# A cross-attention and gated feed-forward kernel: instruction order at the start, the queues of the attention results, and the form of the down projection

## The chip, the cores and the metric

The kernel runs on one core of a Trainium2 chip. A core has a matrix engine (TensorE, PE in the profile, with its weight loads as PEld), a vector engine (VectorE, DVE), an activation engine (ScalarE, ACT), a general engine (GpSimd, POOL) and a queue engine (SyncE, SP). Each runs its own instructions in order and waits for the others by semaphores. DMAs are issued from the instruction streams of SP, ACT or POOL: an instruction that waits there holds back everything behind it, DMAs among them. The metric is the device time of one execution, in microseconds (us).

## What is computed

Eight sequences of 128 tokens with 512 features, all float32: cross attention with 32 heads of 128, then a feed-forward block with 1376 inner features.

```
h   = rmsnorm(layernorm(x)) * ln_weight
q, k, v = h @ w_q.T, ctx @ w_k.T, ctx @ w_v.T          # 32 heads x 128 each
p   = softmax(q k^T + position_bias, masked)
x1  = x + layernorm(x) + (p v) @ w_out.T
y   = layernorm(x1)
g   = silu((y @ Wg.T) * ag) * ((y @ Wu.T) * au)         # 1024 x 1376
out = x1 + (g @ Wd.T) * ad                              # 1024 x 512
```

## The kernel before

**Products.** A float32 matrix product takes two passes through PE, so each matmul in the code stands as two instructions in the profile. Nearly all projections use a seven-product scheme: both operands are cut in 2 x 2 blocks, seven products of sums of blocks replace eight of blocks. The sums of the left operand are made by `sums_a` (L215, four operations: `s1`, `s2`, a difference written over `a21`, and `s4`), those of the right by `sums_b` (L223: `t1`, `t2`, a difference over `b12`, and `t4`). `combine_rows` (L231) makes the sums of a weight tile on GpSimd, `combine_tokens` (L239) those of the tokens on VectorE, with `b12` on GpSimd. `seven` (L248) yields once for each product and tile, in the order 2, 1, 6, 7, 4, 5, 3 with two tiles each, so 14 times; products 2, 6, 7 and 4 are copied out by ScalarE (L259, L269), 1, 5 and 3 added by VectorE (L264, L275). Product 6 needs `s2` and `t2`, product 7 the differences over `a21` and `b12`.

**Start.** The loads are issued by hand on SP and ACT (L131 to L147). `kv(0)` (L396) makes the keys and values of the first of eight groups of four heads, 28 yields; between them the loop at L417 runs `norm1` (L183) and `norm1_T` (L202) for each block of 128 tokens. `norm1` takes mean and variance, a reciprocal deviation, the normed row `y` on VectorE, its square sum on ScalarE, a second reciprocal deviation and the scaled row `hn`; `norm1_T` transposes it on PE into `hT`. The queries of all eight groups follow (L437) and are stored in DRAM.

**Attention.** For each group g and block b, `probabilities` (L316) adds bias and mask on GpSimd (L320), the scores on VectorE (L328), and does the softmax on DVE and ACT. `transpose_p` (L355) turns p by a 32 x 32 transpose on DVE (L358), one DMA to DRAM (`turned`, L360) and four back (`pT`, L365), all on SP. Three blocks later `attend` (L377) multiplies with the values, copies by ScalarE (L386) and writes `att` to DRAM by SP (L387). Meanwhile PE makes the next group's keys and values. In the last group PE does the output projection of the first pair of blocks instead: `out_products(0)` takes a step for each group, after `attended(g, 0)` (L478) has loaded `att` back into `a` (L480, SP) and made its sums on DVE; `load_wo` (L455) loads the output weights and makes their sums on GpSimd. The other three pairs follow (L640), their loads also by `attended`.

**Feed-forward.** Five slices of 256 inner features go through `seven` for gate and up (L724), with the weight sums on GpSimd and `gated` (L687) for the slice before; the last 96 features are done plainly in `last_slice`. Each 128 inner features have an `act` tile. The down projection (L762) is plain: for each block of tokens 11 matmuls of 512 columns, then two operations on VectorE (times `ad`, plus `x1`) and a write; the last block is done in two halves.

**Order.** The kernel's text gives priorities; the framework's scheduler orders each engine's and queue's instructions by its own estimate of when each is ready. `InOrder` (L37) pins an instruction behind all that are traced before it on its engine; before the change, it is used for PE in the last group (which is why those matmuls are all recorded at L45). Tiles of a pool with the same tag share its buffers: `acts` has 18, `work` has several tags with two to four.

Of the kernel before, what the change touches and what calls it, by code (L numbers as in the profile page):

```python
# [17 lines left out]
P = 128  # L18
# [31 lines left out]
def xattn_ffn_kernel(  # L50
# [97 lines left out]

    lnw_sb = const.tile([P, DC], F32, name="lnw_sb")
# [33 lines left out]
    def norm1(b):  # L183
        st = small.tile([P, nc.vector.BN_STATS_DIM], F32, tag="st", name=f"st_{b}")
        xb = x_in[b // 2][:, b % 2, :]
        moments(mv1, b, st, xb)
        rs = rs1[:, b : b + 1]
        rstd_of(rs, mv1[:, b, 1:2], 1.0)
        y = work.tile([P, D], F32, tag="s", name=f"y_{b}", bufs=3)
        nc.vector.tensor_scalar(  # L190
            y, xb, mv1[:, b, 0:1], rs, ALU.subtract, ALU.mult
        )
        sq = work.tile([P, D], F32, tag="aT", name=f"sq_{b}")
        ss = small.tile([P, 1], F32, tag="ss", name=f"ss_{b}")
        nc.scalar.activation(sq, y, AF.Square, accum_out=ss)
        rr = small.tile([P, 1], F32, tag="rr", name=f"rr_{b}")
        rstd_of(rr, ss, 1.0 / D)
        hn = work.tile([P, D], F32, tag="pT", name=f"hn_{b}", bufs=4)
        nc.scalar.activation(hn, y, AF.Copy, scale=rr)
        return b, hn  # L200

    def norm1_T(b, hn):  # L202
        tp = transposed(hn, ps_tp.tile([P, DC, P], F32, tag="pt", name="tp"))
        nc.vector.tensor_tensor(
# [26 lines left out]
    def combine_rows(name, w):  # L231
# [5 lines left out]
        return sums_a(nc.gpsimd, a11, a12, a21, a22, s1, s2, s4)  # L237

    def combine_tokens(src):  # L239
# [6 lines left out]
        return sums_b(nc.vector, b11, b12, b21, b22, t1, t2, t4, nc.gpsimd)  # L246

    def seven(name, tiles, product, part, pool, tag="mm"):  # L248
# [13 lines left out]
        for t in tiles:  # L262
            product(1, t, m[t], True)
            nc.vector.tensor_tensor(part(1, 1, t), part(1, 1, t), m[t], ADD)  # L264
            yield
# [6 lines left out]
        for i, r, c in ((5, 2, 2), (3, 1, 2)):  # L272
            for t in tiles:
                product(i, t, m[t], i == 5)
                nc.vector.tensor_tensor(part(r, c, t), part(r, c, t), m[t], ADD)  # L275
                yield
# [100 lines left out]
    def attend(g, b, pT, v):  # L377
# [9 lines left out]
        nc.sync.dma_start(att[g][b // 2][:, b % 2], aT)  # L387
# [8 lines left out]
    def kv(g, out):  # L396
# [3 lines left out]
        keys = project_T(f"k{g}", combine_rows(f"k{g}", wk), ctx_t, kT)  # L400
# [3 lines left out]
        else:  # L404

            yield from itertools.islice(keys, 4)
            values = project_V(f"v{g}", combine_rows(f"v{g}", wv), ctx_t, v, ps, "sc")
            yield from itertools.islice(values, 4)
            yield from keys
# [4 lines left out]
    ctx_t = combine_tokens(ctx_sb)  # L414
    kvs = {}
    normed = []
    for n, _ in enumerate(kv(0, kvs)):  # L417
        if n % 2 == 1 and 5 <= n < 5 + 2 * B:
            normed.append(norm1((n - 5) // 2))
        if n % 2 == 1 and 11 <= n < 11 + 2 * B:  # L420
            norm1_T(*normed.pop(0))
    for n in normed:
        norm1_T(*n)
    h_t = combine_tokens(hT)

    res_scale = const.tile([P, B], F32, name="res_scale")
    res_bias = const.tile([P, B], F32, name="res_bias")
    nc.vector.tensor_scalar_add(res_scale, rs1, 1.0)
# [391 lines left out]
```

## Time and profile before

| | us |
|---|---|
| median of three runs | 1146.57 (1145.29 to 1150.09) |
| the profiled execution | 1144.65 |
| its span in the profile | 1142.9 |

The profile shows one execution. Where its time goes, by stages of the span (busy us of each engine):

| stage | from, to | PE | DVE | ACT | POOL |
|---|---|---|---|---|---|
| first loads, first product | 0 to 10.91 | 5.7 | 0.7 | 1.0 | 2.5 |
| keys, values, first norm | 10.91 to 68.25 | 50.9 | 33.3 | 23.4 | 30.3 |
| queries | 68.25 to 260.5 | 192.3 | 36.9 | 38.8 | 43.0 |
| attention, groups 0 to 6 | 260.5 to 700 | 438.3 | 258.3 | 187.0 | 152.0 |
| last group, first output pair | 700 to 780 | 70.9 | 49.5 | 19.0 | 28.7 |
| other output pairs | 780 to 926.9 | 146.9 | 52.2 | 9.7 | 14.1 |
| gate and up | 926.9 to 1063.3 | 135.5 | 60.8 | 38.7 | 27.8 |
| down projection | 1063.3 to 1142.9 | 75.8 | 13.5 | 0.1 | 0.0 |

Matmuls are pipelined and their ends are modelled, so a busy PE is not always at its full rate: the time from one start to the next tells the rate. Waits are put down to what came last by semaphore. In groups of waits, the columns are the total, how often, and the longest; in a timeline, the start and the duration.

### The profile page before, as it was taken

How to read it: one execution, taken by the hardware profiler on the slowest of the kernel's cores; microseconds unless marked ns; L12 is line 12 of the kernel's file. 1: busy time of each engine (PE TensorE's matmuls, PEld its weight loads, DVE VectorE, ACT ScalarE, POOL GpSimd, SP SyncE). 2: the span in 40 equal slices, each digit the busy share in tenths (PEclk: the TensorE clock that was granted, in tenths of full speed). 3: DMA queues.
4: the chain of work that ended last, by engine and by line, in shares of the span. 5: the costliest groups of instructions: out<-in, count | busy, mean ns of one | idle time of the engine just before them, and what ended most of it. 6: DMA issues, size and time to landing. Idle time of an engine off the chain costs nothing.

```text
span 1142.9 us, 12312 instructions
## 1 busy us (share of the span) xinstructions
PE 1116.1 (98%) x4286; PEld 729.4 (64%) x4286; DVE 505.2 (44%) x957; ACT 317.5 (28%) x899; POOL 298.4 (26%) x255
## 2 busy tenths in 40 slices
PE   7899999999999999999999999889999999999998
PEld 3564444445867778685868679778888864444445
DVE  4541111116555565555555767653434342434311
ACT  2511112223343444443443443221000022233000
POOL 5531221116333333332311633510000314220000
PEclk9999999999999999999999999989999999999999
DMA  9114433257646555565555466765232602110000
GB/s 281 47 37 146 177 119 111 110 183 263 181 133 208 157 184 167 175 194 168 178 166 165 144 193 217 228 198 159 90 104 63 227 8 74 37 37 1 18 28 28
DMA packets 117533, 154.38 MB, mean 135 GB/s; under 512 B 12032, under 2 KB 71680, under 8 KB 117472
## 3 DMA queue, kind: packets, MB, share of 16 engines
q1 hardware_dynamic: 114784, 149.93, 41.0%
q10 hardware_dynamic: 2192, 2.10, 0.6%
q0 software_dynamic: 496, 1.58, 0.5%
q8 instruction: 34, 0.56, 0.2%
q14 instruction: 27, 0.22, 0.1%
HBM read 101.14 MB, written 52.43 MB: 134 GB/s over the span
## 4 chain that ended last, share of the span: by engine, by line
PE 90%; DVE 4%; DMA 3%; ACT 1%; issue 1%; POOL 0%; SPq 0%; ACTq 0%; DVEq 0%; POOLq 0%
PE mm_q L285 17%; PE mm_v L303 16%; PE mm_k L285 14%; PE m L500 13%; PE mm_f L739 9%; PE dn L770 7%; PE sc L325 4%; PE m L45 4%; PE av L381 4%; DMA a<-att 1%; DMA wv<-in_wvT_dram 1%; ACT s L335 1%; PE av L45 1%; PE tp L176 1%; PE gp L704 1%
## 5 line engine op out<-in xcount | busy, mean ns | idle before, releaser
L320 POOL TENSOR_TENSOR s<-pb,mneg 128x512 f32<-128x512 f32 x64 | 81.6, 1275 | 278.9 <-DVE tt L358 238.6
L285 PE MATMUL mm_k<-ctx_sb,wk 128*128 128x512 f32 x256 | 119.4, 610 | 8.8 <-DMA wk<-in_wkT_dram 4.7
L303 PE MATMUL mm_v<-wv,ctx_sb 128*128 128x256 f32 x512 | 115.9, 379 | 0.5 <-DMA wv<-in_wvT_dram 0.5
L285 PE MATMUL mm_q<-hT,wq 128*128 128x512 f32 x256 | 112.5, 592 | 0.0
L335 ACT ACTIVATE s<-s,nmx 128x128 f32<-128x128 f32 x256 | 99.5, 390 | 34.5 <-DVE nmx L332 34.5
L303 PEld LDWEIGHTS mm_v<-wv,ctx_sb 128*128 128x128 f32 x512 | 95.3, 190 | 14.5 <-DMA wv<-in_wvT_dram 1.3
L386 ACT COPY aT<-av 128x512 f32<-128x512 f32 x64 | 37.5, 585 | 210.9 <-issue 125.4
L285 PE MATMUL mm_k<-ctx_sb,S_k 128*128 128x512 f32 x192 | 87.2, 598 | 3.6 <-POOL S_k L218 2.6
L285 PEld LDWEIGHTS mm_q<-hT,wq 128*128 128x128 f32 x256 | 48.6, 190 | 60.8 <-issue 60.7
L285 PEld LDWEIGHTS mm_k<-ctx_sb,wk 128*128 128x128 f32 x256 | 47.6, 195 | 62.5 <-issue 42.1
L303 PE MATMUL mm_v<-S_v,ctx_sb 128*128 128x256 f32 x384 | 86.7, 381 | 0.0
L285 PE MATMUL mm_q<-hT,S_q 128*128 128x512 f32 x192 | 85.0, 592 | 0.0
L328 DVE TENSOR_TENSOR s<-sc,s 128x512 f32<-128x512 f32 x64 | 44.1, 689 | 85.6 <-PE sc L325 73.8
L303 PEld LDWEIGHTS mm_v<-S_v,ctx_sb 128*128 128x128 f32 x384 | 71.6, 190 | 10.5 <-DVE v L275 1.5
L770 PE MATMUL dn<-wd,act 128*128 128x512 f32 (+3 forms) x198 | 75.8, 545 | 0.0
L275 DVE TENSOR_TENSOR q<-q,mm_q 128x512 f32<-128x512 f32 x32 | 22.0, 687 | 114.9 <-PE mm_q L285 114.9
L500 PE MATMUL m<-wo,a 128*128 128x256 f32 x300 | 72.6, 379 | 0.0
L325 PEld LDWEIGHTS sc<-k,q 128*128 128x128 f32 x448 | 58.7, 192 | 14.8 <-issue 13.4
L285 PEld LDWEIGHTS mm_q<-hT,S_q 128*128 128x128 f32 x192 | 36.5, 190 | 45.9 <-issue 45.9
L285 PEld LDWEIGHTS mm_k<-ctx_sb,S_k 128*128 128x128 f32 x192 | 35.0, 190 | 47.6 <-issue 35.4
L770 PEld LDWEIGHTS dn<-wd,act 128*128 128x128 f32 (+1 forms) x198 | 37.6, 190 | 38.5 <-issue 37.4
L500 PEld LDWEIGHTS m<-wo,a 128*128 128x128 f32 x300 | 56.5, 190 | 7.4
(168 smaller groups left out, 1609.5 us busy)
## 6 DMA issues: line engine op xcount, KB each, us to landing
queries<-q SPq DMA_DIRECT2D x32, 512.0 KB, 3.7
q<-queries SPq DMA_DIRECT2D x32, 512.0 KB, 4.4
turned<-tt SPq DMA_DIRECT2D x64, 256.0 KB, 2.2
pT<-turned SPq DMA_DIRECT2D x256, 64.0 KB, 2.4
att<-aT SPq DMA_DIRECT2D x64, 256.0 KB, 2.3
a<-att SPq DMA_DIRECT2D x32, 512.0 KB, 3.4
wq<-in_wqT_dram SPq DMA_DIRECT2D x8, 1024.0 KB, 5.4
wk<-in_wkT_dram SPq DMA_DIRECT2D x7, 1024.0 KB, 5.8
```

The source lines that it names most:

```text
L45: return self.tc.keep_in_program_order(getattr(self.engine, op)(*args, **kw))
L285: nc.tensor.matmul(out, w[i][:, c, bass.ts(t, P)], src[i][:, c, :], start=(first and c == 0), stop=(c == HC - 1), skip_group_check=True,)
L303: nc.tensor.matmul(out[:, bass.ts(k, HW)], src[i][:, c, bass.ts(2 * t + k, S)], w[i][:, c, :], start=(first and k == 0 and c == 0), stop=( ...
L320: nc.gpsimd.tensor_tensor(s, pb, mneg[:, b : b + 1, :].to_broadcast([P, GH, S]), ALU.add)
L325: tensor.matmul(sc[:, j, :], qT[:, j, bass.ts(b % 2, S)], kT[j][:, cols], start=True, stop=True)
L328: nc.vector.tensor_tensor(s, sc, s, ALU.add)
L335: nc.scalar.activation(s[:, j, :], s[:, j, :], AF.Exp, bias=nmx[:, j : j + 1], accum_out=sm[:, j : j + 1],)
L381: tensor.matmul(av[:, j, :], v[b // 2][:, b % 2, bass.ts(j, P)], pT[:, :, j, :], start=True, stop=True,)
L386: nc.scalar.copy(aT, av)
L500: tensor.matmul(m[n], sa[n][:, c, :], wo_t[g][n][:, c, :], start=(g == order[0] and c == 0 and k % 2 == 0), stop=(g == order[-1] and c == ...
L739: nc.tensor.matmul(out, ws[t][n][:, c, :], h2_t[n][:, c, :], start=(first and c == 0), stop=(c == HC - 1), skip_group_check=True,)
L770: nc.tensor.matmul(o, act[ic][:m, bass.ts(b, S)], wd[:m, ic, cols], start=(n == 0), stop=(n == NI - 1),)
```

## The change

Three things are changed.

At the start, `vector` and `gpsimd` are in-order handles from before the first norm until the query sums are made. All of `norm1`, the token sums, the weight sums of the first keys and values, and the additions of `seven` go through them. The token sums are no longer made at once but at fixed yields. `norm1` is split: `norm1_moments` takes mean and variance and one root; `norm1_scale` makes `hn` from x in one pass of ScalarE, with both norms' deviations in one factor: var(y) is var / (var + EPS), so 1 / sqrt(var (1 + EPS) + EPS^2) is their product. `rs1` for the residual is made once for all blocks.

In the attention, the write of `att` is issued by ScalarE, and the loads of `a` for the first pair of blocks (i = 0) by GpSimd.

The down projection is a seven-product form over the ten full chunks of inner features: blocks b and b + 4 of the tokens are the row halves, even and odd chunks the inner halves, 256 columns each the column halves. The last 96 features are added into four of the accumulators plainly. `weigh_down` multiplies the weights by `ad` and makes their sums on GpSimd, one operation at each yield of slices 1 to 3; `a_sums` makes the activations' sums on VectorE; `down` issues the matmuls, `down_out` adds up the result. The eighth accumulator holds only the last chunk's part. The `act` tiles of even and odd chunks are joined into one tile each, and `sg` takes its buffers from `work`.

```diff
...
+    vector, gpsimd = InOrder(tc, nc.vector), InOrder(tc, nc.gpsimd)
...
-    def norm1(b):
+    def norm1_moments(b):
         st = small.tile([P, nc.vector.BN_STATS_DIM], F32, tag="st", name=f"st_{b}")
         xb = x_in[b // 2][:, b % 2, :]
-        moments(mv1, b, st, xb)
-        rs = rs1[:, b : b + 1]
-        rstd_of(rs, mv1[:, b, 1:2], 1.0)
-        y = work.tile([P, D], F32, tag="s", name=f"y_{b}", bufs=3)
-        nc.vector.tensor_scalar(
-            y, xb, mv1[:, b, 0:1], rs, ALU.subtract, ALU.mult
-        )
-        sq = work.tile([P, D], F32, tag="aT", name=f"sq_{b}")
-        ss = small.tile([P, 1], F32, tag="ss", name=f"ss_{b}")
-        nc.scalar.activation(sq, y, AF.Square, accum_out=ss)
+        vector.bn_stats(st, xb)
+        vector.bn_aggr(mv1[:, b, :], st)
         rr = small.tile([P, 1], F32, tag="rr", name=f"rr_{b}")
-        rstd_of(rr, ss, 1.0 / D)
+        vector.tensor_scalar(rr, mv1[:, b, 1:2], 1.0 + EPS, EPS * EPS, ALU.mult, ALU.add)
+        nc.scalar.activation(rr, rr, AF.Sqrt)
+        return b, rr
+    def norm1_scale(b, rr):
+        xb = x_in[b // 2][:, b % 2, :]
+        vector.reciprocal(rr, rr)
+        nm = small.tile([P, 1], F32, tag="nm", name=f"nm_{b}")
+        vector.scalar_tensor_tensor(nm, mv1[:, b, 0:1], -1.0, rr, ALU.mult, ALU.mult)
         hn = work.tile([P, D], F32, tag="pT", name=f"hn_{b}", bufs=4)
-        nc.scalar.activation(hn, y, AF.Copy, scale=rr)
+        nc.scalar.activation(hn, xb, AF.Identity, bias=nm, scale=rr)
         return b, hn
...
-        nc.vector.tensor_tensor(
+        vector.tensor_tensor(
...
-        return sums_a(nc.gpsimd, a11, a12, a21, a22, s1, s2, s4)
-    def combine_tokens(src):
+        return sums_a(gpsimd, a11, a12, a21, a22, s1, s2, s4)
+    def token_sums(src):
...
-        return sums_b(nc.vector, b11, b12, b21, b22, t1, t2, t4, nc.gpsimd)
+        sums = [
+            partial(vector.tensor_tensor, t1, b12, b11, SUB),
+            partial(vector.tensor_tensor, t2, b22, t1, SUB),
+            partial(gpsimd.tensor_tensor, b12, b22, b12, SUB),
+            partial(vector.tensor_tensor, t4, b21, t2, SUB),
+        ]
+        return {1: b11, 2: b21, 3: b22, 4: t4, 5: t1, 6: t2, 7: b12}, sums
...
-            nc.vector.tensor_tensor(part(1, 1, t), part(1, 1, t), m[t], ADD)
+            vector.tensor_tensor(part(1, 1, t), part(1, 1, t), m[t], ADD)
...
         nc.scalar.copy(aT, av)
-        nc.sync.dma_start(att[g][b // 2][:, b % 2], aT)
+        nc.scalar.dma_start(att[g][b // 2][:, b % 2], aT)
...
-        keys = project_T(f"k{g}", combine_rows(f"k{g}", wk), ctx_t, kT)
+        rows_k = combine_rows(f"k{g}", wk)
+        keys = project_T(f"k{g}", rows_k, ctx_t, kT)
         if g:
             yield from keys
             yield from project_V(f"v{g}", combine_rows(f"v{g}", wv), ctx_t, v, ps_mm)
         else:
-            yield from itertools.islice(keys, 4)
+            ctx_sums[0]()
+            yield from itertools.islice(keys, 3)
+            ctx_sums[1]()
+            ctx_sums[2]()
+            yield from itertools.islice(keys, 1)
             values = project_V(f"v{g}", combine_rows(f"v{g}", wv), ctx_t, v, ps, "sc")
             yield from itertools.islice(values, 4)
+            ctx_sums[3]()
             yield from keys
             yield from values
...
-    ctx_t = combine_tokens(ctx_sb)
+    ctx_t, ctx_sums = token_sums(ctx_sb)
     kvs = {}
-    normed = []
+    normed, transposed1 = [], 0
+    scales = []
     for n, _ in enumerate(kv(0, kvs)):
-        if n % 2 == 1 and 5 <= n < 5 + 2 * B:
-            normed.append(norm1((n - 5) // 2))
-        if n % 2 == 1 and 11 <= n < 11 + 2 * B:
+        if n in (3, 6, 8, 9, 10, 12, 14, 16):
+            scales.append(norm1_moments(len(scales) + len(normed) + transposed1))
+        if n in (6, 8, 9, 10, 12, 14, 16, 18):
+            normed.append(norm1_scale(*scales.pop(0)))
+        if n in (10, 11, 12, 14, 16, 18, 20, 22):
             norm1_T(*normed.pop(0))
-    for n in normed:
-        norm1_T(*n)
-    h_t = combine_tokens(hT)
+            transposed1 += 1
+    h_t, h_sums = token_sums(hT)
+    for form in h_sums:
+        form()
+    vector, gpsimd = nc.vector, nc.gpsimd
...
+    rstd_of(rs1, mv1[:, :, 1], 1.0)
...
     def attended(g, i):
         a = acts.tile([P, 2, GH, S], F32, tag="a", name=f"a_{g}_{i}")
-        nc.sync.dma_start(a, att[g][i])
+        (nc.sync if i else nc.gpsimd).dma_start(a, att[g][i])
...
-    act = [actp.tile([P, T], F32, tag="act", name=f"act_{ic}") for ic in range(NI)]
+    act_even, act_odd = (
+        actp.tile([P, NP, T], F32, tag=f"act{k}", name=f"act_{k}") for k in range(2)
+    )
+    act_rest = actp.tile([P, T], F32, tag="act2", name="act_2")
+    act = [(act_odd if ic % 2 else act_even)[:, ic // 2, :] for ic in range(NI - 1)] + [act_rest]
...
+    def weigh_down(wd):
+        tiles = [
+            work.tile([P, 2, HW], F32, tag=tag, name=f"T_d{k}", bufs=n)
+            for k, (tag, n) in enumerate(t_tags)
+        ]
+        spare = iter([t[:, h] for t in tiles for h in range(2)])
+        for n in range(1, 8):
+            wd_t[n] = []
+        for ic in range(NI):
+            m = min(P, INTER - ic * P)
+            yield partial(gpsimd.tensor_tensor, wd[:m, ic], wd[:m, ic], ad_sb[:m], ALU.mult)
+            if ic % 2:
+                b11, b12 = wd[:, ic - 1, :HW], wd[:, ic - 1, HW:]
+                b21, b22 = wd[:, ic, :HW], wd[:, ic, HW:]
+                t1, t2, t4 = next(spare), next(spare), next(spare)
+                for n, t in enumerate((b11, b21, b22, t4, t1, t2, b12)):
+                    wd_t[n + 1].append(t)
+                yield partial(gpsimd.tensor_tensor, t1, b12, b11, SUB)
+                yield partial(gpsimd.tensor_tensor, t2, b22, t1, SUB)
+                yield partial(gpsimd.tensor_tensor, b12, b22, b12, SUB)
+                yield partial(gpsimd.tensor_tensor, t4, b21, t2, SUB)
...
-    def gated(act, gate, up, ic, m, sg):
+    def gated(act, gate, up, ic, m):
+        sg = work.tile([P, 512], F32, tag="pT", name=f"sg_{ic}", bufs=4)[:m]
         nc.scalar.activation(sg, gate, AF.Sigmoid, scale=ag_sb[:m, ic : ic + 1])
...
         if i == 0:
             wd = load_down()
+            gpsimd = InOrder(tc, nc.gpsimd)
+            down_sums = list(weigh_down(wd))
...
+            if 0 < i < NP - 1 and down_sums:
+                down_sums.pop(0)()
         for r in range(2):
             ic = 2 * i + r
-            sg = acts.tile([P, T], F32, tag="a", name=f"sg_{ic}")
...
-    for b in range(B):
-        r = work.tile([P, D], F32, tag="aT", name=f"r_{b}")
-        parts = 1 if b + 1 < B else 2
-        for k in range(parts):
-            cols = bass.ts(k, D // parts)
-            o = ps.tile([P, D // parts], F32, tag="m", name=f"dn_{b}_{k}")
-            for n, ic in enumerate([NI - 1, *range(NI - 1)]):
-                m = min(P, INTER - ic * P)
-                nc.tensor.matmul(
-                    o, act[ic][:m, bass.ts(b, S)], wd[:m, ic, cols],
-                    start=(n == 0), stop=(n == NI - 1),
-                )
-            nc.vector.tensor_tensor(r[:, cols], o, ad_sb[:, cols], ALU.mult)
-            nc.vector.tensor_tensor(r[:, cols], r[:, cols], x1[b // 2][:, b % 2, cols], ALU.add)
-            nc.sync.dma_start(out[b][:, cols], r[:, cols])
...
+    def a_sums(b, parts):
+        s = [acts.tile([P, NP, S], F32, tag="a", name=f"S{k}_d{b}") for k in range(3)]
+        up, dn = bass.ts(b, S), bass.ts(b + HB, S)
+        for sl in parts:
+            sums_a(
+                nc.vector, act_even[:, sl, up], act_odd[:, sl, up],
+                act_even[:, sl, dn], act_odd[:, sl, dn], *(t[:, sl, :] for t in s),
+            )
+        return {
+            1: act_even[:, :, up], 2: act_odd[:, :, up], 3: s[2], 4: act_odd[:, :, dn],
+            5: s[0], 6: s[1], 7: act_even[:, :, dn],
+        }
+    LAST = {2: (0, 0), 3: (0, 1), 4: (1, 0), 8: (1, 1)}
+    ORDER = (2, 1, 6, 7, 4, 5, 8, 3)
...
+    def down(b, sa, last):
+        names = [(2, 1), (6, 7), (4, 5)] + ([(8,), (3,)] if last else [(8, 3)])
...
+        todo = [(n, i) for n in ORDER for i in range(-1, NP)]
+        if b == 0:
+            todo.sort(key=lambda ni: ni[1])
+        todo = [(n, i) for n, i in todo if (n in LAST if i < 0 else n < 8)]
...
+        for n, i in todo:
+            out, _ = m[n]
...
+            if i < 0:
+                r, c = LAST[n]
+                lhs = act_last[:m_last, bass.ts(b + r * HB, S)]
+                rhs = w_last[:m_last, bass.ts(c, HW)]
+            else:
+                lhs, rhs = sa[n][:, i, :], wd_t[n][i]
+            nc.tensor.matmul(
+                out, lhs, rhs, start=bank not in started,
+                stop=(i == NP - 1 or n == 8), skip_group_check=True,
+            )
...
+    def down_out(b, m, both, last):
+        r1, r2 = x1[b // 2][:, b % 2, :], x1[(b + HB) // 2][:, b % 2, :]
...
+        nc.scalar.copy(u[:, 0], m[1])
+        nc.vector.tensor_tensor(r1[:, :HW], r1[:, :HW], m[2], ADD)
+        nc.gpsimd.tensor_tensor(r1[:, :HW], r1[:, :HW], u[:, 0], ADD)
+        nc.vector.tensor_tensor(u[:, 1], u[:, 0], m[6], ADD)
+        nc.vector.tensor_tensor(w, u[:, 1], m[7], ADD)
+        nc.gpsimd.tensor_tensor(r1[:, HW:], r1[:, HW:], u[:, 1], ADD)
+        nc.vector.tensor_tensor(r2, r2, both[:].rearrange("p a n -> p (a n)"), ADD)
+        nc.vector.tensor_tensor(
+            r2.rearrange("p (a n) -> p a n", a=2), r2.rearrange("p (a n) -> p a n", a=2),
+            w.unsqueeze(1).to_broadcast([P, 2, HW]), ADD,
+        )
+        nc.vector.tensor_tensor(r1[:, HW:], r1[:, HW:], m[5], ADD)
+        nc.vector.tensor_tensor(r2[:, HW:], r2[:, HW:], m[8], ADD)
+        nc.sync.dma_start(out[b + HB], r2)
+        if last:
+            nc.sync.dma_start(out[b][:, :HW], r1[:, :HW])
+        nc.vector.tensor_tensor(r1[:, HW:], r1[:, HW:], m[3], ADD)
+        nc.sync.dma_start(*((out[b][:, HW:], r1[:, HW:]) if last else (out[b], r1)))
+    sa = a_sums(0, (slice(0, NP - 1), slice(NP - 1, NP)))
+    for b in range(HB):
+        coming = a_sums(b + 1, (slice(0, NP),)) if b + 1 < HB else None
+        last = b + 1 == HB
+        down_out(b, *down(b, sa, last), last)
+        sa = coming
```

## The prediction

> **What bounds the kernel now.** I read the page's busy totals and 40 slices first. TensorE (PE) is busy 98% of the span: a gain must give it less work or close its gaps. The slices with gaps are the first three, one after 700 us, and the last.
>
> ```profile
> PE 1116.1 (98%) x4286; PEld 729.4 (64%) x4286; DVE 505.2 (44%) x957; ACT 317.5 (28%) x899; POOL 298.4 (26%) x255
> PE   7899999999999999999999999889999999999998
> ```
>
> Then the busy times by stage, for the three that the change touches: keys, values and first norm (10.91 us, where the first loads have landed, to the first query product at 68.25), the last attention group (700 to 780), and the down projection. Columns: PE, weight loads, DVE, ACT, POOL, granted clock, DMA.
>
> ```profile
> 10.91:68.25 57.34, 50.86 (x192) 33.91 (x193) 33.32 (x83) 23.42 (x58) 30.30 (x21) 0.97 0.45 135
> 700.00:780.00 80.00, 70.90 (x370) 62.78 (x369) 49.48 (x100) 19.01 (x69) 28.68 (x23) 0.94 0.65 202
> 1063.30:1142.90 79.60, 75.82 (x199) 37.38 (x197) 13.47 (x21) 0.06 (x1) 0.00 (x0) 0.99 0.07 27
> ```
>
> Next, what PE waited for (total, times, longest). The first two lines are of the first stage, the next two of the last group; the last three are SP's waits in that group.
>
> ```profile
> PE mm_k L285 <- ACT k L269: 3.4, 1, 3.4
> PE mm_k L285 <- POOL S_k L218: 2.6, 1, 2.6
> PE m L45 <- DMA a<-att: 7.7, 2, 4.5
> PE m L45 <- DVE S_a L218: 1.4, 1, 1.4
> SPq L387 <- ACT aT L386: 15.4, 8, 3.8
> SPq L365 <- DMA turned<-tt: 12.4, 7, 2.6
> SPq L360 <- DVE S_a L217: 12.2, 3, 4.3
> ```
>
> The last fact is SP's order in time before the worst waits. The load `a` that PE starts on at 721.86 is issued at 716.90, behind four pT loads, a write that waits for DVE, and an `att` write whose data was ready at 711.54. The one for 753.49 stands behind pT loads too.
>
> ```profile
> 713.17 1.74 SPq L365 DMA_DIRECT2D pT<-turned  x4
> 716.04 0.34 SPq L360 DMA_DIRECT2D turned<-tt  x1
> 716.48 0.38 SPq L387 DMA_DIRECT2D att<-aT  x1
> 716.90 0.46 SPq L480 DMA_DIRECT2D a<-att  x1
> ...
> 747.63 1.75 SPq L365 DMA_DIRECT2D pT<-turned  x4
> 749.42 0.44 SPq L480 DMA_DIRECT2D a<-att  x1
> ```
>
> **Part 1: keys, values, first norm (kept order).** A pass of 512 columns takes 0.429 us (192.27 us for 448 in the chain), one of 256 takes 0.216 (42.30 for 196). After 10.91 us this stage still has 48 key passes (56 less the 8 done), 112 value passes of 256, and eight transposes at 0.44 (60.80 less 60.36): 20.6 + 24.2 + 3.5 = 48.3 us of the 57.3. **9.0 us** is there to win: waits of 3.4, 2.6 and 0.5, the rest passes at half speed after them.
>
> The 2.6 is POOL's: S_k L217 (15.02), then S_v L217 (2.31 us) and the token sum L227 (3.33 us) before S_k L218, which PE needs. Kept order puts all four S_k sums together: 1.69 + 3 x 1.35 after 15.02 = 20.8, the second done at 18.1, while PE wants it at 21.4. Then comes the token sum `b12`, 2.35 (L227 on hT) to 3.33 us: done at 23.1 to 24.1; product 7 wants it at 24.9. The cover is under 2 us; without it PE waits by as much as the sum is late. S_v's two first sums follow, by 27; values' product 6 comes at 39.
>
> The 3.4 is ACT's: a key copy came at 31.26 because ACT was in the norm. Per block the new norm drops `y` (DVE 0.92), Square and its read (ACT 0.62 + 0.19), the second deviation (DVE 0.14 + 0.16, ACT 0.20), and adds `nm` (DVE, by the nearest row 0.15); the hn pass stays at about 0.72. Times eight: ACT loses 8 us, DVE 8.6. Still, at yields 8 to 10 ACT has a copy (0.57), a root (0.20) and an hn pass (0.72), 1.5 of the 1.72 us that PE needs for a product, and DVE's fixed order makes a reciprocal wait for the additions traced before it. PE can stand a copy some 1 us late. The one new 128x8 deviation costs 0.35 us on idle engines. The four query sums at the end need DVE 1.2 to 3.0 us each for two, under four query products (6.9 us), as before.
>
> Bounds: -9.0 (no wait left) to -3 (copies and `b12` late by a microsecond several times). I take 2 us of remaining waits, as little slack is left in two places: **-7**.
>
> **Part 2: `att` writes on ACT, first-pair `a` loads on POOL.** 64 writes leave SP; ACT pays about 0.37 us each (the SP row; ACT's own issues at the start took 0.37 to 0.51), 24 us over 317 busy of 1143. In groups 0 to 6 PE is full, so neither this nor SP's relief is on the path; behind each write stand the next exponentials, 0.4 us later, under a lag of three blocks. A write waits only for ACT's own copy, no longer for SP.
>
> In the last group the passes at half speed add to the gaps: 8 + 4 + 4 passes after 753.49 took 6.6 us for 3.45, those after 721.86 about 1.8 too long. So 9.1 + 3.2 + 1.8 = **14 us** are lost there. Eight loads move to POOL. A load issued there takes POOL 0.75 to 0.79 us and lands later, by the rows of 512 KB weight loads (median us to landing):
>
> ```profile
> wg<-in_wgT_dram SPq DMA_DIRECT2D x3, 512.0 KB, 3.7
> wg<-in_wgT_dram POOLq DMA_DIRECT2D x1, 512.0 KB, 5.8
> ```
>
> A rule speaks against this edit. The Trainium skill, "DMA: Bandwidth & Descriptors", section "Rules for kernel authors", says that spreading DMAs over SP, ACT and GpSimd brings no bandwidth, only issue time. By it eight loads save 8 x 0.4 us of SP and land 2.1 us later each: nothing, or up to +4 for the two that PE waits for. The rows weigh more: what is lost is not bandwidth (DMA is busy 0.65 there) but the place behind other waits, up to 5 us a time. POOL was idle from 712.36 to 717.14. Issued at 712.4, the load lands at 718.2; PE is ready at about 718.5: the first wait (3.2 + 1.8) goes. Issued before L225 at 741.87, the second lands by 748 and its 4.5 + 3.2 go. But POOL has its own waits, behind any of which a load can stand: L320 waits for DVE's tt (21.1 us in all), the `wo` sums for their loads (13.2 us). If the second stands behind L228 (749.32 + 1.26) it lands at 757, later than now, unless the second half of the last `wo`, issued at 742.22 behind an `att` write, comes sooner, which the edit allows: then about 753, no gain.
>
> Bounds: -13 (all but 1 us) to +21 (rival C). Near rows favour POOL's idle time for the first load and leave the second open; I take all of the first wait's 5: **-5**. Next late after that is the score-softmax-transposition chain by DVE.
>
> **Part 3: down projection by seven products.** Before: eight blocks x 11 chunks of 512 columns, two passes each (154 of 512 and, the last block being halved, 44 of 256): 75.6 us. After, per pair of blocks, 7 products x 5 chunk pairs + 4 of the last chunk = 39 of 256 columns, two passes each; four pairs: 312 x 0.2158 = 67.3. **-8.3 us.**
>
> Beside it: POOL gets 11 multiplications 128x512 (1.26) and 20 sums 128x256 (0.72), 28 us, in the gate/up slices where it is busy 24 of 123 us. The weights landed at 915. Fourteen (13 us) stand before the next slice's sums (6.4 us): 955 + 13 + 6.4 = 975, due at about 990. DVE's gatings that overlap POOL take 2.1 instead of 1.4 us, DVE being 42% busy. Nothing is hidden only barely. DVE also gets 16 activation sums: 12 of 128x640 (0.82 between the 512 and 1024 rows), 10 us, each four under 16.8 us of products. Only the first four are exposed: DVE ends its gatings at 65.5 (1065.5), the seven products reach their first sum at 1063.3 + 8 x 0.216 + 4 x 0.216 = 1065.9; two sums of 0.69 behind the gatings make PE wait 1.2 us, nothing if they go into DVE's gaps, 2.5 if all four are late. I take 1. `sg` in another pool and the joined `act` tiles cost nothing: four buffers serve gatings made two at a time; if they were short, DVE's slack pays.
>
> The end: now 3.8 us pass from the last pass to the span's end (0.42 + 0.42 on DVE, then a 128 KB write). After, one addition less (-0.4), but 384 KB more of output are issued just ahead of the last 128 KB; at 1.7 to 2.1 us for 256 KB this gives -0.4 to +1.5; I take 0. Sum: **-7.3** (-8.7 to -4.3).
>
> **Sum.** -7 - 5 - 7.3 = -19.3: span 1142.9 to 1123.6. Around it lie 1.75 us (1144.65 - 1142.9): 1125.4; the median of the runs is 1.9 above the profiled execution: **1127**.
>
> **Rivals.**
> - A, the forecast: 1127; its own range 1122 to 1132. Chance 0.50.
> - B, GpSimd's queue waits where SP's did (L320 waits for the same tt), so part 2 gives nothing: -14.3, 1132. For it: 21.1 us of such waits; against: the idle time at 712. Chance 0.22.
> - E, all gaps close: -9 - 13 - 8.3 = -30, 1116. Against it: the thin cover in part 1. Chance 0.14.
> - D, the pinned start stalls (-3), part 3 yields -4.3, part 2 nothing: 1139. Chance 0.08.
> - C, slower: `a` loads on POOL stand behind the `wo` sums. Behind L228 at 723.3 one lands at 723.3 + 0.8 + 5.8 = 729.9 instead of 721.86 (+8); behind 734.4 at 741 for a step that began at 731.4 (+9.6); behind 750.6 at 757.2 (+3.7): +21, less 14.3 = +7, 1153. It decides once more than two loads stand so. Against it: those sums wait for loads issued about when `a` is. Chance 0.06.
>
> That the change doesn't do what it says (the order not kept) is in B and D.
>
> The range 1116 to 1138 leaves out C, half of E and most of D, 0.17. Half a percent (5.7 us) is what a measurement here can tell from no change; A, B and E are faster, D is split: faster 0.90, same 0.05, slower 0.05.
>
> **What would show it.** Part 1: no PE wait for S_k or the copies, first query product at 59 to 63. Part 2: `a` loads issued by POOL between 708 and 714 and before 742; PE waits for `a` below 4 us. Part 3: 312 passes, 67 us, from the last gate/up product to the end about 72. Wrong would be: PE waits on `b12` at 25, POOL's sums ahead of `a`, gate/up products waiting for S_g behind POOL's new work.

## The result and the profile after

The changed kernel takes **1131.6 us** (median of 4 runs, 1130.9 to 1135.3) against 1146.1 before (4 runs, 1145.3 to 1150.1): a ratio of 0.9873, 95% interval 0.9841 to 0.9905. The forecast was 1127, in a range of 1116 to 1138. The profiled execution of the changed kernel took 1130.87, its span is 1129.1: 13.8 us shorter than before.

The first view shows the page of the changed kernel: busy totals, TensorE's row of the 40 slices, and TensorE's granted clock.

```profile
PE 1102.5 (98%) x4400; PEld 750.8 (66%) x4400; DVE 527.2 (47%) x977; ACT 315.5 (28%) x880; POOL 344.2 (30%) x302
PE   7999999999999999999999998988999999999998
PEclk9999999999999999999999999998999999999999
```

The start is full from the second slice on. After 700 us the gap sits later (the 27th and 28th slice, 734 to 790), and a new one stands at 677 to 706; the row of the clock dips in the 28th. Next, the same three stages as before the change, by busy time (columns: the stretch and its length, then PE, weight loads, DVE, ACT, POOL, granted clock, DMA share, GB/s). In the last group TensorE is idle for 7.7 us, against 9.1 before.

```profile
10.91:61.78 50.87, 48.65 (x192) 33.66 (x193) 29.89 (x67) 18.10 (x35) 27.80 (x20) 1.00 0.48 150
697.85:768.63 70.78, 63.09 (x346) 56.82 (x345) 49.70 (x98) 18.25 (x68) 30.26 (x27) 0.96 0.68 220
1058.28:1129.10 70.82, 67.54 (x313) 59.03 (x311) 29.27 (x55) 2.65 (x6) 5.77 (x8) 1.00 0.08 30
```

And what TensorE waits for in the changed kernel (total, times, longest). Of the lines shown of before, the waits for `S_k`, `a` and `S_a` are gone. In their place stand waits for the transposed probabilities `pT`, for value additions, and for additions of the gate and up stage.

```profile
PE av L45 <- DMA pT<-turned: 7.7, 2, 7.4
PE mm_v L314 <- DVE v L286: 3.3, 2, 1.9
PE mm_f L796 <- DVE gate L275: 2.4, 3, 1.4
PE mm_k L296 <- ACT k L280: 2.1, 2, 1.9
PE mm_f L796 <- DVE act L275: 1.4, 3, 0.7
PE mm_q L296 <- DVE q L275: 0.7, 1, 0.7
```

From the times of TensorE's first instruction of each stage follows where the 13.8 us come from:

| stage | before, us | after, us | difference |
|---|---|---|---|
| start to the first query product | 68.25 | 61.78 | -6.5 |
| queries of all groups, to the keys of group 1 | 193.2 | 194.1 | +1.0 |
| to the first output product (groups up to the last) | 441.5 | 442.0 | +0.5 |
| last group with the first output pair | 76.35 | 70.78 | -5.6 |
| the other output pairs, second norm | 147.7 | 149.6 | +1.9 |
| gate and up | 136.4 | 140.0 | +3.6 |
| down projection and end | 79.6 | 70.8 | -8.7 |

So parts 1 and 2 give about what was forecast inside their stages, by size. But 7 us are given back in four places that the change was expected not to touch.

### The profile page after: what moved, and what is told of

Same layout as the page of the kernel before. It is cut to its first block, busy times and chain, and to the rows that moved or that the text cites. A ratio compares the mean times of both kernels' runs of the same rounds, so it can differ in the third digit from the quotient of the medians.

```text
span 1129.1 us, 12623 instructions
## 1 busy us (share of the span) xinstructions
PE 1102.5 (98%) x4400; PEld 750.8 (66%) x4400; DVE 527.2 (47%) x977; ACT 315.5 (28%) x880; POOL 344.2 (30%) x302
## 3 DMA queue, kind: packets, MB, share of 16 engines
q0 software_dynamic: 1648, 5.77, 1.6%
## 4 chain that ended last, share of the span: by engine, by line
PE 84%; DVE 7%; DMA 4%; issue 2%; ACT 2%; POOL 1%; SPq 0%; ACTq 0%; POOLq 0%; DVEq 0%
PE mm_q L296 16%; PE mm_v L314 16%; PE mm_k L296 15%; PE m L524 13%; PE mm_f L796 8%; PE d L874 6%; PE sc L336 4%; PE av L392 4%; DMA a<-att 2%; DVE sg L745 1%; ACT s L346 1%; DMA wv<-in_wvT_dram 1%; DVE act L748 1%; PE gp L759 1%; PE up L759 1%
## 5 line engine op out<-in xcount | busy, mean ns | idle before, releaser
L314 PE MATMUL mm_v<-wv,ctx_sb 128*128 128x256 f32 x512 | 118.2, 379 | 1.3 <-DMA wv<-in_wvT_dram 1.3
L336 PEld LDWEIGHTS sc<-k,q 128*128 128x128 f32 x448 | 62.7, 191 | 21.7 <-issue 19.6
L339 DVE TENSOR_TENSOR s<-sc,s 128x512 f32<-128x512 f32 x64 | 44.0, 688 | 67.4 <-PE sc L336 66.9
L336 PE MATMUL sc<-k,q 128*128 128x128 f32 x448 | 63.1, 275 | 0.0
L392 PE MATMUL av<-pT,v 128*128 128x128 f32 x424 | 56.0, 275 | 0.0
```

The source lines that it names most:

```text
L314: nc.tensor.matmul(out[:, bass.ts(k, HW)], src[i][:, c, bass.ts(2 * t + k, S)], w[i][:, c, :], start=(first and k == 0 and c == 0), stop=( ...
L336: tensor.matmul(sc[:, j, :], qT[:, j, bass.ts(b % 2, S)], kT[j][:, cols], start=True, stop=True)
L339: nc.vector.tensor_tensor(s, sc, s, ALU.add)
L392: tensor.matmul(av[:, j, :], v[b // 2][:, b % 2, bass.ts(j, P)], pT[:, :, j, :], start=True, stop=True,)
```

## The experiments

All medians are of the runs made in the study; the kernel before was run beside them each time (1146.0 to 1146.5).

**1. Part 1 without its order.** The shorter norm and the spread sums stay where they are traced.

```diff
-    vector, gpsimd = InOrder(tc, nc.vector), InOrder(tc, nc.gpsimd)
+    vector, gpsimd = nc.vector, nc.gpsimd
```

> The changed kernel with the start's in-order handles replaced by the plain engines; the shorter norm and the spread token sums stay. Theory 1 (the fixed order brings the gain): the S_k sums on GpSimd fall back behind S_v and the token sum, PE waits again 2 to 4 us before product 6, and the first query product comes at 65 to 68 us instead of 61.8. Theory 2 (the shorter norm and the spacing of the token sums bring it): the first query product stays at 61 to 63 us, and the loss of 0.9 us in the first query products, which comes from the pinned query sums, goes, so that the time falls by about 1 us.

Measured: 1144.1 us, ratio 0.9979 [0.9967, 0.9992]; first query product at 73.63. That is 5.4 us later than in the kernel before and 11.9 later than in the changed one. Its waits in the first stage, in TensorE's view:

```profile
PE mm_k L296 <- ACT k L280: 4.9, 1, 4.9
PE mm_v L314 <- ACT v L270: 2.6, 1, 2.6
PE mm_v L314 <- DVE v L286: 2.1, 1, 2.1
```

Neither theory came out as written. TensorE's wait for `S_k` did not come back: GpSimd still made the second `S_k` sum by 20.9, with one `S_v` sum and no token sum ahead of it. What came instead are waits for copies, behind roots and scaled rows on ScalarE, and for additions behind the query sums on VectorE. So the later place of the token sums is enough to remove the wait for `S_k`, and the kept order removes the others. The kept order is worth 12.5 us against this version, and without it the edit loses at the start. Whether the shorter norm would gain alone, with the old places of its steps, was not tried.

**2. Part 2 in its four combinations.** Three kernels: SP writes `att` (ScalarE's queue otherwise), SP loads the first pair's `a` (GpSimd otherwise), and both.

```diff
-        nc.scalar.dma_start(att[g][b // 2][:, b % 2], aT)
+        nc.sync.dma_start(att[g][b // 2][:, b % 2], aT)
-        (nc.sync if i else nc.gpsimd).dma_start(a, att[g][i])
+        nc.sync.dma_start(a, att[g][i])
```

> The changed kernel with the writes of att issued by SP again, the first pair's loads still by GpSimd. Theory 1 (the place of the writes in SP's queue held up what stood behind them): in the last group the transposed probabilities and the output weights are late, PE waits by 2 to 5 us more than in the changed kernel. Theory 2 (only the loads of a matter): the last group keeps its length within 1 us. Either way groups 0 to 6 stay within 1 us, since PE is full there.

> The changed kernel with the first pair's a loads issued by SP again, the writes still by ScalarE. Theory 1 (the loads' place in SP's queue was the loss): PE waits again some 4 to 8 us for a, the time rises by 3 to 6 us. Theory 2 (taking the writes off SP is enough): no wait for a over 1 us and the same time. The wait of 7.4 us for the last pT goes only if the loads on GpSimd caused it; I expect it to stay in some form, because VectorE waits 5 us for a load of the second pair ahead of the last softmax, and that load is SP's in either kernel.

> The changed kernel with both halves of part 2 taken back: SP writes the attention results and SP fetches the first pair's `a`, as in the kernel before; parts 1 and 3 stay. It is the fourth corner beside the changed kernel (1131.6 us), SP's writes alone (1133.8) and SP's loads alone (1125.8). Theory 1, the writes on ScalarE's queue are what gains, because a load behind them in SP's order starts late: the last group is back at 75 to 76 us (70.8 in the changed kernel, 71.2 with the loads on SP), with TensorE waits of 7 us or more for `a`, and the time is 1132 to 1135. Theory 2, the loads on GpSimd are a plain loss and the writes' queue makes no difference: the time is that of SP's loads alone, 1125 to 1127.

| median, us | `a` loaded by GpSimd | `a` loaded by SP |
|---|---|---|
| `att` written by ScalarE | 1131.6 (changed kernel) | **1125.8** |
| `att` written by SP | 1133.8 | 1133.9 |

Moving the writes to ScalarE's queue gains 8 us when SP loads `a`; with the loads on GpSimd the 2.2 us are within the spread of the runs. Moving the loads to GpSimd gains nothing in either row and costs 5.7 in the upper one. SP's loads with ScalarE's writes give a ratio of 0.9810 [0.9785, 0.9835] to the kernel before; its interval lies wholly below that of the changed kernel.

In the last group itself either move alone shortens the stage: it takes 74.9 us with both by SP, 71.6 with only the loads moved, 71.2 with only the writes, 70.8 with both. What the loads cost stands in other stages. TensorE's waits in the last group, with both by SP:

```profile
PE m L45 <- DMA a<-att: 8.4, 3, 5.4
PE m L45 <- DVE S_a L223: 0.7, 1, 0.7
PE m L45 <- DVE a L224: 0.3, 1, 0.3
```

and with only the writes moved:

```profile
PE m L45 <- DMA a<-att: 6.0, 2, 3.6
```

The move of the writes also takes 2.4 us off the groups before. In SP's queue its waits for ScalarE's copies, 10.6 us between 672 and 770, are gone with it; that this is the whole cause of the 8 us is likely, but not shown.

The trace shows where GpSimd's loads cost. In the changed kernel's timeline of VectorE (start, duration, instruction, and in brackets the idle time before it with its releaser), the sums of the first `a` stand at the head of VectorE's order and the load has not landed:

```profile
686.79 0.42 DVE L222 TENSOR_TENSOR S_a<-a 128x256 f32<-128x256 f32 x1 [5.74 <-DMA a<-att]
...
691.24 0.68 DVE L339 TENSOR_TENSOR s<-sc,s 128x512 f32<-128x512 f32 x1
...
693.51 0.68 DVE L286 TENSOR_TENSOR v<-v,mm_v 128x512 f32<-128x512 f32 x1
```

Value additions are queued behind those 5.7 us, and so TensorE waits the 3.3 us for `v` shown above. With the loads on SP the same sums wait 1.1 us in the groups up to the last, and that wait of TensorE is gone: the groups take 438.8 us in place of 442.0, the other output pairs 147.7 in place of 149.6. The other kernels of this study agree. In all seven with the writes on ScalarE's queue and the loads on GpSimd, the changed one among them, VectorE waits 3.3 to 5.7 us for the first `a` and TensorE 1.1 to 3.3 us for `v`, the groups take 439.5 to 443.1, the other output pairs 148.2 to 149.6. In all three with the same writes and the loads on SP, TensorE has no such wait, and the stages take 437.8 to 439.0 and 147.7. But the engine that issues is not the whole of it: with the writes on SP, VectorE waits 2.1 us with GpSimd's loads and 2.2 with SP's, and TensorE for `v` in neither. In the timeline of GpSimd the sixth of the eight loads stands behind the sums of `wo`, as rival C had it, though only this one stands behind all four:

```profile
728.29 1.27 POOL L231 TENSOR_TENSOR wo<-wo,wo 128x512 f32<-128x512 f32 x1
729.52 1.27 POOL L232 TENSOR_TENSOR wo<-wo,wo 128x512 f32<-128x512 f32 x1
730.74 1.26 POOL L233 TENSOR_TENSOR wo<-wo,wo 128x512 f32<-128x512 f32 x1
731.95 0.56 POOL L504 DMA_DIRECT2D a<-att  x1
```

**3. The plain down projection.** The down projection of the kernel before in place of part 3, with no weights to multiply on GpSimd; `sg` stays in its new place.

```diff
-            down_sums = list(weigh_down(wd))
...
-            if 0 < i < NP - 1 and down_sums:
-                down_sums.pop(0)()
-    for b in range(HB):
...
-        down_out(b, *down(b, sa, last), last)
+    for b in range(B):
...
+                nc.tensor.matmul(
+                    o, act[ic][:m, bass.ts(b, S)], wd[:m, ic, cols],
+                    start=(n == 0), stop=(n == NI - 1),
+                )
```

> The changed kernel with the plain down projection of before, and without GpSimd's multiplications and sums of the down weights; act tiles and sg as in the change. Theory 1 (GpSimd's new work slows VectorE in the gate and up slices[...]): the waits of 3.8 us in that stage fall to 1 or less, and the down projection takes 75.6 us again, so the time rises by 8.3 + 0.5 - 3 = about 6 us. Theory 2 (the new place of sg lets the gatings run in one burst ahead of the additions): the 3.8 us stay, and the time rises by about 9 us.

Measured: 1139.1 us, 7.5 more than the changed kernel, ratio 0.9941 [0.9920, 0.9962]. The down projection takes 79.5 us again, but the gate and up stage only falls from 140.0 to 139.0. So GpSimd's new work alone was not the main reason of the 3.6 us there. (It makes 11 multiplications in that stage, not the 22 that a later expectation names.)

**4. `sg` back in a tile of `acts` for each row block**, first alone, then together with the plain down projection.

```diff
-        sg = work.tile([P, 512], F32, tag="pT", name=f"sg_{ic}", bufs=4)[:m]
...
+            sg = acts.tile([P, T], F32, tag="a", name=f"sg_{ic}")
```

> The changed kernel with the sigmoid's tile `sg` back in a [128 x 1024] tile of the acts pool, one for each row block, as in the kernel before, in place of [128 x 512] tiles in the shared four buffers of `pT`. Theory 1, the gate and up stage's 3.6 us (136.4 before, 140.0 changed) come from where sg lives and when the gatings then run: TensorE's waits for the gate additions and for act fall from 3.8 us to 1 or less, the stage takes 136.5 to 137.5 and the run is 3 us shorter, 1128 to 1129. Theory 2, they come from the 22 multiplications and the sums of the down weights that GpSimd does in that stage: the stage stays at 139 to 140 and the time at 1131 to 1132.

> The changed kernel with the plain down projection of the kernel before (so that GpSimd has no down weights to multiply and sum) and sg back in the acts pool: with the two suspects for the gate and up stage's 3.6 us both taken away. The stage took 136.4 us before, 140.0 changed, 139.0 with the plain down projection alone, 138.3 with sg's place alone. Theory 1, the two share it and are separate: 136.4 to 137.2, TensorE's waits for the gate additions and act at 1 us or less. Theory 2, something else of the change (what the seven-product form does to the work pool, or the kept order's effect on the planner) holds part of it: 138 or more. The time of the whole is 1136 to 1138 by theory 1, 1138 to 1140 by theory 2.

Measured: alone 1130.6 us (1126.5 to 1134.1, not to be told from the changed kernel), stage 138.3. Together 1138.3 us, stage 136.45, which is the 136.4 of the kernel before. So both causes are at work, and each alone hides a part of the other: taking away GpSimd's work gives back 1.0 us, the place of `sg` 1.7, both together 3.6. These are stages of single profiles; in seven kernels that have both causes the stage takes 139.5 to 141.4, in three with `sg` moved and GpSimd's work kept 138.3 to 138.5, so the 1.0 by itself is hardly clear of the scatter. TensorE's waits for these additions fall from the 3.8 us shown above to this one line with both taken back:

```profile
PE mm_f L794 <- DVE gate L275: 1.0, 3, 0.3
```

How it comes about is in VectorE's timeline, in the changed kernel

```profile
956.87 0.95 DVE L745 SCALAR_TENSOR_TENSOR sg<-gate,ag_sb,sg 128x512 f32<-128x512 f32 x1 [0.79 <-ACT sg L744]
...
958.35 1.16 DVE L745 SCALAR_TENSOR_TENSOR sg<-gate,ag_sb,sg 128x512 f32<-128x512 f32 x1
959.43 2.88 DVE L748 SCALAR_TENSOR_TENSOR act<-act,au_sb,sg 128x512 f32<-128x512 f32 x2
962.24 1.21 DVE L745 SCALAR_TENSOR_TENSOR sg<-gate,ag_sb,sg 128x512 f32<-128x512 f32 x1
963.49 1.10 DVE L748 SCALAR_TENSOR_TENSOR act<-act,au_sb,sg 128x512 f32<-128x512 f32 x1
964.50 0.67 DVE L275 TENSOR_TENSOR gate<-gate,mm_f 128x512 f32<-128x512 f32 x1
```

and in the one with both taken back:

```profile
960.95 2.12 DVE L744 SCALAR_TENSOR_TENSOR sg<-gate,ag_sb,sg 128x512 f32<-128x512 f32 x2 [2.27 <-ACT sg L743]
962.99 1.40 DVE L747 SCALAR_TENSOR_TENSOR act<-act,au_sb,sg 128x512 f32<-128x512 f32 x2
964.31 0.67 DVE L275 TENSOR_TENSOR gate<-gate,mm_f 128x512 f32<-128x512 f32 x1
```

The addition L275 that TensorE waits for stands behind three gatings in place of two, and most of their passes take 1.1 to 1.4 us, in place of 0.7 to 1.1: GpSimd multiplies down weights beside the first of them and makes the next slice's sums beside the rest. In the changed kernel the addition is then late for the next product, by 1.4 us here; in the other by 0.3.

**5. The wait for the last `pT`.** In the changed kernel the chain of waits (start, duration, what) through that stretch runs like this:

```profile
747.45 5.92 DMA a<-att
...
753.39 0.43 DVE S_a L222
753.82 0.59 DVE mx L341
...
758.35 0.70 DVE tt L369
...
759.08 3.10 DMA turned<-tt
...
763.63 3.03 DMA pT<-turned
...
766.80 2.04 PE av L45 x8
```

VectorE stands for the second pair's `a`, and the last block's softmax is behind it. So these sums were put behind the last block's transposition; then, in a second kernel, ScalarE's two residual scalings also behind the last block's exponentials.

```diff
+        with tc.issue_after(last_tt[-1].ins) if i == 1 else ExitStack():
+            return sums_a(
...
```

The second adds:

```diff
+            with tc.issue_after(last_exp[-1].ins) if i == 0 else ExitStack():
+                nc.scalar.activation(
+                    x1[i][:, k, :], x1[i][:, k, :], AF.Identity,
...
```

> The changed kernel with one thing moved: VectorE's sums of the second pair's `a` are put behind the transposition of the last attention block in VectorE's order; the queues stay as they are. Theory 1, the new 7.4 us wait of TensorE for the last pT begins when VectorE stands 5 us for that `a` with the last block's softmax queued behind it: the wait for pT falls to 2 us or less, the last group takes 64 to 66 us in place of 70.8, TensorE then waits 0 to 3 us for the second pair's sums, and the time falls by 3 to 6 us, 1126 to 1129. Theory 2, the wait is the DMA's own (queue or bandwidth of the blocks' transposed writes): the wait stays at 6 us or more and the time at 1131 to 1132.

> The changed kernel with VectorE's sums of the second pair's `a` behind the last block's transposition, and now also ScalarE's two residual scalings (which wait for x from HBM) behind the last block's exponentials; the queues stay as in the changed kernel. With the first edit alone the wait for the last pT stayed at 7.7 us, since ScalarE stood 4.3 us for x with the exponentials behind it. Theory 1, the wait for pT is what is left of the last block's softmax after whatever it is queued behind: with both gone it falls to 4 us or less, and the last group to 67 to 69 us (70.8 and 72.0). Theory 2, the wait is the two DMA trips of the turned block (9.4 us from the transposition to av) and their place in SP's order: it stays at 6 us or more and the last group at 70 or more.

Measured: 1132.3 us (1128.2 to 1134.1) and 1130.7 (1129.7 to 1133.1); the wait for the last `pT` is 7.7 and 5.3 us (in the second with 2.0 us for `a` besides), the last group 72.0 and 71.9. Neither is faster than the changed kernel, so the theory that VectorE's place alone causes the wait fell. In the first, ScalarE stands instead, as its timeline shows: the exponentials, ready at 749.6, come at 753.01.

```profile
749.18 0.81 ACT L658 ACTIVATE x<-x,res_bias,res_scale 128x512 f32<-128x512 f32 x1 [2.96 <-DMA x<-in_x_dram]
751.32 0.81 ACT L658 ACTIVATE x<-x,res_bias,res_scale 128x512 f32<-128x512 f32 x1 [1.33 <-DMA x<-in_x_dram]
...
753.01 0.40 ACT L346 ACTIVATE s<-s,nmx 128x128 f32<-128x128 f32 x1 [0.40 <-ACT aT L398]
```

In the second, the transposition ends at 757.3 (756.55 + 0.71). SP then writes it out only at 760.65, since its fixed order has the `pT` loads of the block before and a load of `a` ahead, and those wait until 758.25 for a write issued at 752.29:

```profile
752.29 0.45 SPq L372 DMA_DIRECT2D turned<-tt  x1
758.25 1.82 SPq L377 DMA_DIRECT2D pT<-turned  x4
760.17 0.39 SPq L505 DMA_DIRECT2D a<-att  x1
760.65 0.38 SPq L372 DMA_DIRECT2D turned<-tt  x1
```

The last block passes through three queues that serve in order, and each carries something that waits for a transfer. One stander freed leaves the next. What removes TensorE's wait for `pT` in the profiles is SP loading `a`; TensorE then waits for `a` earlier (6.0 us in two waits), and the last group is no shorter (71.2). How low all of these could go together stays open.

**6. Versions meant to be the fastest.** The first has `a` on SP, `sg` in `acts` and the second pair's sums behind the last transposition. The second also takes the token sums of the queries out of the kept order.

```diff
-    h_t, h_sums = token_sums(hT)
-    for form in h_sums:
-        form()
     vector, gpsimd = nc.vector, nc.gpsimd
+    h_t, h_sums = token_sums(hT)
+    for form in h_sums:
+        form()
```

> Three edits to the changed kernel together: SP fetches all of `a` (the writes stay on ScalarE's queue), sg is back in the acts pool, and the second pair's sums stand behind the last block's transposition. If each removes its own wait, the gains add: 5.7 for the loads, 3 for sg, and at most 2 for the order of the sums, which has little left to remove once no pT wait is there: 1121 to 1123, and 0.979 or less of the kernel before. If the loads' gain and the sums' order are the same wait, the sum is 1122 to 1124. If sg gains nothing, 1125 to 1126.

> The fastest of the versions so far (loads of `a` on SP, sg in the acts pool, the second pair's sums behind the last transposition: 1125.6 us) with one more edit: the token sums of the queries' hT are no longer tied to the order written out, so that VectorE may put the first query additions among them. Theory 1, the 0.7 us wait of TensorE after the first query products comes from that order: it goes, and the time is 0.5 to 1 us lower, 1124.5 to 1125. Theory 2, the sums themselves are late whatever their order: the wait stays, 1125.5, or grows, as the planner puts the sums later.

Measured: 1125.6 us (ratio 0.9821 [0.9800, 0.9842]) and 1126.5 (0.9831 [0.9814, 0.9847]). Both beat the changed kernel, by as much as SP's loads alone do: the other two edits add nothing that can be told. Without the kept order for the query sums the first query product comes at 67.94, not at 61.68: VectorE forms the sums (5.77 us) ahead of value additions, and TensorE waits 2.1 us for those with passes at half speed after it. Of these 6.3 us, 2.2 are there by 33 us already, where the two kernels do the same; some 4 are the order's. Later 1.0 us comes back in the queries, 1.2 in the groups and 2.8 in the last group (68.7 us in place of 71.4); why the last two do is not shown. So the 0.7 us wait after the first query products is the small price of an order that saves some 4 us in front of it, most of which is lost later.

## Why the prediction was right, and where not

The direction and the range were right, and so is the bulk of the mechanism in parts 1 and 3. The sum was 5.5 us too large by the profile (19.3 forecast, 13.8 found). That it came out at rival B's 1132 is not rival B's doing: each of the three parts gave less by the stages, and in the last group part 2 gave something (70.8 us, and 74.9 with it taken back). Over the whole kernel its 2.3 us are within the spread of the runs, so B's number for part 2, nothing, is not excluded by them.

- **Part 1: -7 forecast, -5.5 found** (-6.5 at the first query product, within the 59 to 63 named, less 1.0 after it). The mechanism holds: the `S_k` wait is gone, `b12` was done at 23.3 and product 7 started at 25.1 without a wait, the clock of the stage rose from 0.97 to 1.00. Mis-sized is the term "`nm` (DVE, by the nearest row 0.15)". Beside GpSimd's sums it took 1.26 to 1.29 us twice, 2.2 us more than forecast in all. The hn pass and the key copy behind it came late, which is enough for the wait of 1.9 us at 29.3; a version without this delay was not run. What the forecast put down to the kept order, that `S_k` comes in time, held without it too (experiment 1). The query sums "as before" were not: tied, they hold up the first query additions. The stage of the queries takes 194.1 us in the ten kernels that keep the tie, and 193.2 in the two without it and in the kernel before.
- **Part 2: -5 forecast, -3.1 found by the stages and -2.3 by the runs** (1133.9 with part 2 taken back). Right: `a` loads were issued at 704.9, 710.4 and 732 to 735, and TensorE no longer waits for `a` in the last group. Wrong is the step that chose the rows over the rule. It credited the loads with the gain, "what is lost is not bandwidth [...] but the place behind other waits", and took GpSimd's idle time as the place. In the last group alone that holds, where the loads moved by themselves are worth 3.3 us. Over the whole kernel the combinations show that the writes on ScalarE's queue gain and the loads on GpSimd lose 5.7 us or nothing. That the last group fell by 5.6 us, near the 5 forecast, is luck: 9.1 us of waits for `a` and `S_a` went, the second long one too, and TensorE's busy time fell by 4.2 us as slow passes went with them; 7.7 us of waits for `pT` came. The rule of the Trainium skill, "DMA: Bandwidth & Descriptors", section "Rules for kernel authors", that a second queue saves only issue time, came nearer for the loads, at "nothing, or up to +4". For the writes the rows' reading came nearer: their move gained 8 us with SP's loads. "Next late after that is the score-softmax-transposition chain" was named, but at no cost; it cost 7.4 us and, by passes at half speed behind it (eight in 3.62 us, where 1.89 is usual), most of the 1.9 us after.
- **Part 3: -7.3 forecast, -5.2 found by the stages and -6.8 by the runs** (1138.3 with its products and the place of `sg` taken back). The down projection itself gave more: from its first pass to the end of the span -8.7, as 312 passes take 67.4 us (forecast 67.3), the 1 us for the first sums did not come, and the end is 0.5 shorter. What failed is "Nothing is hidden only barely" and "`sg` in another pool [...] cost nothing": they cost 3.6 us, shared by the place of `sg` and by GpSimd's work. The expected sign was products waiting for `S_g`; they waited for additions behind gatings instead.
- **Rivals.** C's mechanism occurred once (731.95) and cost no wait of its own on TensorE. B's cause, GpSimd's own waits, is partly what the loads met: two of them stand at 679.2 behind a wait of 4.6 us for `tt`. D and E did not happen.

## What to carry to other kernels

Count a moved DMA at both ends: what the queue that loses it can now do sooner, and what stands in the fixed order of the engine that waits for its data, since a late load at the head of VectorE's order delays everything queued behind it. When a wait is removed from a chain that passes through several in-order queues, price the next one before booking the gain. And what a change only moves to another buffer or an idle engine needs its own check of the order that follows: here 3.6 us came from a place for `sg` and an engine with time to spare.

## What the hardware did that was not expected

A VectorE instruction on 128 single elements took eight times as long while GpSimd was working. In the changed kernel's timelines, GpSimd's sums and `nm`:

```profile
26.67 1.27 POOL L45 TENSOR_TENSOR wv<-wv 128x512 f32<-128x512 f32 x1
```

```profile
26.69 1.26 DVE L45 SCALAR_TENSOR_TENSOR nm<-mv,rr 128x1 f32<-128x1 f32 x1
...
29.06 0.16 DVE L45 SCALAR_TENSOR_TENSOR nm<-mv,rr 128x1 f32<-128x1 f32 x1
```

It begins with GpSimd's instruction and ends with it; at 29.06, just before GpSimd's next one, it takes 0.16. This agrees with the Trainium skill, "SBUF — State Buffer", section "Who interferes with whom": a VectorE instruction with two inputs from SBUF contends with a GpSimd instruction that reads SBUF, and the order of issue decides which of the two is held up. Here GpSimd's came first, by 0.02 us. So what this instruction cost was set by its neighbour, not by its size.

Short waits of TensorE were sometimes followed by a lower clock and sometimes not. After the same wait for a key copy, in a stage where the two kernels do the same, four passes took 1.98 us with only `sg` moved back, and 3.36 with SP's loads:

```profile
29.24 1.98 PE L296 MATMUL mm_k<-ctx_sb,wk 128*128 128x512 f32 x4 [2.17 <-ACT k L280]
```

```profile
29.44 3.36 PE L296 MATMUL mm_k<-ctx_sb,wk 128*128 128x512 f32 x4 [2.18 <-ACT k L280]
```

The granted clock from there to 31.0 was 1.00 in the first, and to 32.6 it was 0.57 in the second. In the changed kernel it was 0.50 from 768.6 to 772.0, after the 7.4 us wait. A stage's time scatters by some 2 us in this way: in the kernels that keep the whole start of the change the first query product comes at 61.7 to 63.6.
